# Graph attention on one core: overflow guard from softmax sums, and when a scheduling lead is given back

## Chip, cores, metric

The kernel runs on one core of a Trainium2 chip. The metric is the device time of one execution in microseconds, as the median of several runs. The engines are named TensorE (PE, with its weight loads as PEld), VectorE (DVE), ScalarE (ACT), GpSimd (POOL) and SyncE (SP, which here only issues DMAs).

## What is computed

One layer of graph attention with a residual and a layer norm, for 16 graphs (the batch) of 1024 nodes, 512 features, 8 heads of 64:

```python
q = (x @ Wq + bq).reshape(b, n, H, HD)
k = (x @ Wk + bk).reshape(b, n, H, HD)
v = (x @ Wv + bv).reshape(b, n, H, HD)
scores = jnp.einsum('bqhd,bkhd->bhqk', q, k) / jnp.sqrt(jnp.float32(HD))
scores = scores + (1.0 - adj)[None, None, :, :] * -1000000000.0
attn = jax.nn.softmax(scores, axis=-1)
out = jnp.einsum('bhqk,bkhd->bqhd', attn, v).reshape(b, n, d)
return _layernorm(x + out @ Wo + bo)
```

One adjacency matrix serves all graphs. It is sparse: an entry is 1 with a chance of about 0.004, more for early nodes. A query without any edge ("lone" below) has a softmax over 1024 equally masked scores; the kernel lets it take the mean of all values.

## The kernel before

**Edges instead of a score matrix.** The kernel sorts the queries by their number of edges (`ranks`, with the result in `asked_row` and `ranked`) and cuts them into 8 tiles of 128. Tile t handles its first `OWN[t]` = 1, 2, 2, 3, 4, 5, 5, 7 edges in "own" blocks, in which partition p is query p; the edges beyond that, of the two last tiles, are packed into 1 and 5 further blocks (`BLOCKS`), whose results are added by a matmul with a 0/1 matrix (`add_up`, lines 906 and 907). That is 29 + 6 = 35 blocks a graph, `NB` = 35, 560 in all, each with 128 edges.

**Front work**, in `pair` and `transpose_x`: x is loaded (SP), transposed on TensorE, multiplied by the weights; q goes to `q_rows` and k beside v to `kv_rows` in DRAM (SP), each of which has `ROWS` = 3 buffers, so that graph b overwrites graph b - 3. k and v come from a scheme with fewer products (lines 670 to 702). `norm` (line 566, ScalarE) squares and sums every row of q and k by pairs of heads, and `mean_pe` takes their maxima into `gmax` (line 623) and writes the mean of v into the extra row N of `kv_rows`.

**Attention work**, one block a step: POOL gathers q rows (line 824 or 834) and k and v rows (line 840) up to `AHEAD` = 8 blocks ahead; `products` (line 857, VectorE), `scores` (line 861, VectorE), `exponentials` (line 871, ScalarE; p is taken without subtracting a maximum), `weigh` (line 881 on ScalarE or line 885 on VectorE), `add_own` (line 897) or `add_up`. `normalise` divides by the sums of p at the end of a tile (lines 915 to 924), then comes a transpose on TensorE (line 932), a copy (936), and `finish`: projection by Wo (line 554), residual, layer norm (lines 762 to 784, with one power on POOL, line 778) and a scattering store (788).

**The order is written out by a planner** in the program, step by step[...]. A step n serves block n; there are 34 steps of lead-in before n = 0. Each step gets a `share` of TensorE time in microseconds, by costs: `PRODUCT` 0.86, `SUM` 0.87, `TRANSPOSE` 0.44. It is spent as `credit` on units of `finishing` (projections) first, and then of `fronts`, until the credit is used up. Functions put off by `later(k, fn)` and `later_last(k, fn)` run k steps on, in `plan` (before ScalarE's weighing) or `rest` (after it); transposes wait in `urgent` and go first. At each graph's first step the share is set so that, at the graph's end, front work is 2 graphs plus a lead ahead. The lead is `EARLY` = 13 steps, and `FIRST` = 11 more at the end of graph 0:

```python
                elif n % NB == 0:

                    left = sum(u[0] for u in fronts)
                    goal = fronts_time - (n // NB + 2 + (EARLY + (FIRST if n < NB else 0)) / NB) * batch_time
                    share = (max(0.0, left - goal) + NT * NPAIR * PRODUCT + NS * SUM) / NB
```

From step 455 on (graph 13) the remaining fronts are spread evenly up to step 513, and the ten tiles in `SPILL` (102 to 111) have their projections put off: their input goes to DRAM and comes back as `oTs` when the fronts are done. After that the share is `LAST_SHARE` = 3.0.

**The guard.** Since no maximum is subtracted, the kernel checks that the scores cannot be large: the greatest norm of q times (greatest norm of k + norm of bk) is at most `LIMIT`. It also checks (the tile `check`) that the matrix holds only 0 and 1 and that all edges fit into the blocks. `guard` runs as a generator, one piece a step from step 521 on, and writes `flag`. If the flag is set, a general program (`tile_general`) computes everything anew. Here it is not set.

Of the kernel before, what the change touches and what calls it, by code (L numbers as in the profile page):

```python
# [10 lines left out]
F32 = mybir.dt.float32  # L11
BF16 = mybir.dt.bfloat16
I32 = mybir.dt.int32
AF = mybir.ActivationFunctionType
OP = mybir.AluOpType
AX = mybir.AxisListType

HEADS = 8
EPS = 1e-5
NEG = 1e9  # L20
LIMIT = 31.0

# [8 lines left out]
LAZY = 2  # L33

SPILL = range(102, 112)
# [5 lines left out]
EARLY = 13  # L41

FIRST = 11
# [10 lines left out]
P = 128  # L54
# [103 lines left out]
def kernel(  # L158
# [32 lines left out]

    nc = tc.nc
    B, N, D = x.shape
    HD = D // HEADS
    NPAIR = D // P
    NT = N // P
    HALF = N // 2
    HD2 = D // 2  # L200
    scale = 1.0 / HD ** 0.5
# [23 lines left out]
    with ExitStack() as main:  # L225
# [6 lines left out]
        def fill_psum(name):  # L232
            return psum.tile([P, HALF], F32, tag="fill", name=name, bufs=4)
# [26 lines left out]
        query_row = one.tile([P, NS], I32, name="query_row")  # L260

        absent = one.tile([P, NB - NS], F32, name="absent")
        check = one.tile([P, 2 * NT], F32, name="check")

        asked, ranked = (one.tile([P, NT, 2], F32, name=name) for name in ("asked", "ranked"))
        key, rank = (one.tile([P, NT], F32, name=name) for name in ("key", "rank"))
        rank_row, asked_row = (one.tile([P, NT], I32, name=name) for name in ("rank_row", "asked_row"))
        ADJ = []
        gmax = one.tile([P, 2 * B], F32, name="gmax")

        kv_rows = [dram.tile([N + 1, 2 * D], F32, name=f"kv_rows_{i}") for i in range(ROWS)]
        q_rows = [dram.tile([N, D], F32, name=f"q_rows_{i}") for i in range(ROWS)]
# [42 lines left out]
        def bias_setup():  # L315
            bk_bc = work.tile([P, D], F32, tag="y", name="bk_bc", bufs=Y_BUFS)
            broadcast(bk_bc, bk)
            yield
            n4 = small.tile([P, NPAIR], F32, name="bk_norms")
            nc.vector.tensor_tensor(bk_bc, bk_bc, bk_bc, op=OP.mult)  # L320
            nc.vector.tensor_reduce(n4, bk_bc.rearrange("p (h d) -> p h d", d=P), axis=AX.X, op=OP.add)
            nc.vector.tensor_reduce(bk_norm, n4, axis=AX.X, op=OP.max)
            yield
            pb = fill_psum("pb")
            nc.tensor.transpose(pb[:, 0:2 * NPAIR], bias_rows, ident[:2 * NPAIR, :2 * NPAIR])
            nc.tensor.transpose(pb[:, 2 * NPAIR:3 * NPAIR], bv_rows, ident[:NPAIR, :NPAIR])
            yield
            nc.vector.tensor_copy(bias_qk, pb[:, 0:2 * NPAIR])
            bv_col = one.tile([P, NPAIR], F32, name="bv_col")
            nc.vector.tensor_copy(bv_col, pb[:, 2 * NPAIR:3 * NPAIR])  # L330
            bvb = work.tile([P, NPAIR, P], F32, tag="y", name="bvb", bufs=Y_BUFS)
            nc.vector.tensor_copy(bvb, bv_col[:, :, None].to_broadcast([P, NPAIR, P]))
            yield
            pb = fill_psum("pb3")
            for c in range(NPAIR):
                nc.tensor.matmul(pb, bvb[:, c, :], W["o"][:, c, :], start=(c == 0), stop=(c == NPAIR - 1))
            yield
            nc.vector.tensor_tensor(bo_bc, pb, bo_bc, op=OP.add)
# [5 lines left out]
        def later(k, fn):  # L344
            plan.setdefault(now[0] + k, []).append(fn)

        def later_last(k, fn):
            rest.setdefault(now[0] + k, []).append(fn)
# [3 lines left out]
        def ranks():  # L352
# [46 lines left out]
            yield  # L399
            yield  # L400
            nc.vector.tensor_copy(asked_row, ranked[:, :, 0])

        def checks():
            for t in range(NT):
# [153 lines left out]

            return [(PRODUCT, lambda c=c: unit(c), None) for c in range(NPAIR)]

        def norm(b, t, i, s):
            if t == 0 and i == 0:
                NRM[b] = work.tile([P, 2, NT, NPAIR], F32, tag="nrm", name=f"nrm_{b}", bufs=2)
            for h in range(NPAIR):
                sq = work.tile([P, P], F32, tag="sq", name=f"sq_{b}_{t}_{i}_{h}", bufs=2)
                nc.scalar.activation(sq, s[:, ts(h, P)], AF.Square, accum_out=NRM[b][:, i, t, h:h + 1])  # L566

        def pair(b, j):

# [7 lines left out]
            def out_q(i, p):  # L577

                assert gathered[0] >= NB * (b - ROWS + 1)
                q = work.tile([P, D], F32, tag="q", name=f"q_{b}_{tt[i]}", bufs=2)  # L580
                nc.vector.scalar_tensor_tensor(q, p, scale, bq_bc, op0=OP.mult, op1=OP.add)  # L581
                later(1, lambda: nc.sync.dma_start(q_rows[b % ROWS][ds(tt[i] * P, P), :], q))
                later_last(1, lambda: norm(b, tt[i], 0, q))

            def out_k(i, p):
                kv = new_kv(i)
                nc.scalar.copy(kv[:, 0:D], p)
                later_last(1, lambda: norm(b, tt[i], 1, kv[:, 0:D]))

            def out_v(i, p):  # L590
                nc.scalar.copy(KV[b, tt[i]][:, D:], p)
# [20 lines left out]
            def mean_pe():  # L612
                p = fill_psum(f"pm_{b}")
                nc.tensor.matmul(p[0:1, :], mean, VSUM.pop(b), start=True, stop=True)

                def out():
                    m = work.tile([1, D], F32, tag="q", name=f"mean_{b}", bufs=2)
                    nc.scalar.copy(m, p[0:1, :])
                    nc.sync.dma_start(kv_rows[b % ROWS][N:N + 1, D:], m)
                    set_up[b] = True  # L620
                    nrm = NRM.pop(b)
                    for i in range(2):
                        nc.vector.tensor_reduce(
                            gmax[:, i * B + b:i * B + b + 1], nrm[:, i, :, :], axis=AX.XY, op=OP.max
                        )

                later(1, out)

# [62 lines left out]
            def out_k1():  # L691
                kv = KV[b, tt[1]]
                nc.vector.tensor_tensor(kv[:, 0:D], R["p4"], R["g"], op=OP.add)
                send(1)
                later_last(1, lambda: norm(b, tt[1], 1, kv[:, 0:D]))

            def out_v1():
                nc.vector.tensor_tensor(new_kv(1)[:, D:], R["z"], R["g"], op=OP.add)  # L698
# [113 lines left out]

        KG, QG, PV, PSUM, QT = {}, {}, {}, {}, {}
        blocks = [(b, t, i) for b in range(B) for t in range(NT) for i in range(OWN[t] + BLOCKS[t])]

        def gather(n):
# [30 lines left out]

        def products(n):  # L850
            b, t, i = blocks[n]
            if i < OWN[t]:
                q = QT[b, t] if i < OWN[t] - 1 else QT.pop((b, t))
            else:
                q = QG.pop(n)
            QK[n] = work.tile([P, D], F32, tag="qk", name=f"qk_{n}", bufs=2)
            nc.vector.tensor_tensor(QK[n], q, KG[n][:, 0:D], op=OP.mult)  # L857
# [51 lines left out]
        def normalise(b, t):  # L909
            pv = PV.pop((b, t))  # L910
            o = work.tile([P, D], F32, tag="o", name=f"o_{b}_{t}", bufs=2)
            r = small.tile([P, HEADS], F32, tag="rden", name=f"rden_{b}_{t}", bufs=2)
            if BLOCKS[t]:
                s = PSUM.pop((b, t))
                nc.vector.tensor_tensor(r, s[:, 1, HD2:HD2 + HEADS], pv[:, D:], op=OP.add)
# [13 lines left out]
            def transpose():  # L929
# [12 lines left out]

                later(1, out)

            later(1, lambda: urgent.append(transpose))
            if not fronts:
                coming.append((b, t))
# [1 line left out]


        def guard():
            g = small.tile([P, 4], F32, name="g")
            for i in range(2):
                nc.vector.tensor_reduce(g[:, i:i + 1], gmax[:, ts(i, B)], axis=AX.X, op=OP.max)
            nc.vector.tensor_reduce(g[:, 2:3], check, axis=AX.X, op=OP.max)
            nc.vector.tensor_copy(g[:, 3:4], bk_norm)
            yield
            pg = fill_psum("pgt")
            nc.tensor.transpose(pg[0:4, 0:P], g, ident)
            yield  # L960
            m = small.tile([4, 1], F32, name="gm")
            nc.vector.tensor_reduce(m, pg[0:4, 0:P], axis=AX.X, op=OP.max)
            yield
            pg = fill_psum("pgt2")
            nc.tensor.transpose(pg[0:1, 0:4], m, ident[0:4, 0:4])
            yield
            r = small.tile([1, 8], F32, name="r")
            nc.vector.tensor_copy(r[:, 0:4], pg[0:1, 0:4])
            yield
            yield  # L970
# [11 lines left out]
            nc.vector.tensor_scalar(r[:, 4:5], r[:, 4:5], LIMIT, None, op0=OP.is_le)  # L982
            nc.vector.tensor_scalar(r[:, 5:6], r[:, 2:3], 0.0, None, op0=OP.is_le)
            nc.vector.tensor_tensor(r[:, 6:7], r[:, 4:5], r[:, 5:6], op=OP.mult)
            nc.vector.tensor_scalar(flag, r[:, 6:7], -1.0, 1.0, op0=OP.mult, op1=OP.add)

        out_rows = {(b, t): out_views[b * NT + t].rearrange("b n d -> (b n) d") for b in range(B) for t in range(NT)}
        done, coming, spilled, gathered, fronts = [], [], [], [0], []

        total = len(blocks)  # L990
        prep = {}
# [2 lines left out]
        prep.setdefault(12 - LEAD_IN, []).append(bias_setup())  # L994
        prep.setdefault(-22, []).append(checks())
        preps = [loads(), ranks()]
        prep.setdefault((B - 1) * NB - 4, []).append(guard())
        with tc.manual_schedule():

            fronts += transpose_x(0, 0) + transpose_x(0, 1)  # L1000
# [8 lines left out]
            for t in range(3):  # L1009
                load_x(0, t)  # L1010
            n = -LEAD_IN
            while n < total or plan or rest or urgent or done or finishing or spilled:
                now[0] = n
                if n < 0:
                    share = LISTS_SHARE if n > -16 else LEAD_SHARE if n > -LEAD_IN else TRANSPOSE * 1.5
                elif n >= SPILL[0] // NT * NB + NB:

                    share = sum(u[0] for u in fronts) / max(fronts_end - n, 1) + NS * SUM / NB if fronts else LAST_SHARE
                elif n % NB == 0:

                    left = sum(u[0] for u in fronts)
                    goal = fronts_time - (n // NB + 2 + (EARLY + (FIRST if n < NB else 0)) / NB) * batch_time
                    share = (max(0.0, left - goal) + NT * NPAIR * PRODUCT + NS * SUM) / NB
                if 0 <= n + 3 < total:
                    exponentials(n + 3)
# [31 lines left out]
                while credit > 0 or urgent:  # L1057
                    if urgent and not (first_unit and fronts):
                        urgent.pop(0)()
                        continue  # L1060
                    if not finishing and len(done) > (LAZY if fronts else 0) and n > loaded.get(done[0], n) + 1 and n > last_finish + 1:
                        finishing = finish(*done.pop(0))
                        last_finish = n
                    units = finishing or fronts
# [56 lines left out]
```

## Time and profile before

| | |
|---|---|
| median of 3 runs | 2012.16 us (2010.32 to 2013.15) |
| profiled execution | 2012.86 us |
| its span, first to last instruction | 2011.1 us |
| granted TensorE clock, mean | 0.988 |
| DMA: moved, mean rate | 563.17 MB, 280 GB/s |
| POOL gathers of k and v, line 840 | 560, 635.8 us busy, 453.5 us idle before them |
| ScalarE weighing, line 881 | 3608, 910.4 us |
| ScalarE squares of q and of k, line 566 | 512 and 512, 151.1 and 150.9 us |

The busy time of an engine counts its instructions, not its waits. Two instructions of one engine can overlap, so that the sum over a group can be more than the group's share of busy time. An fp32 matmul stands in the trace as two passes. Idle time is put down to what ended it.

### The profile page before, as it was taken

The page shows a single profiled execution, that of the slowest core. Times are in us where ns is not written, and L with a number is a line of the kernel's source. Part 1 is how long each engine was busy: PE and PEld are TensorE (multiplying, and loading weights), DVE is VectorE, ACT ScalarE, POOL GpSimd, SP SyncE. Part 2 cuts the span into 40 slices and gives each one's busy share as a digit, 9 for nine tenths or more (in the row PEclk, how much of TensorE's full clock was granted, in tenths as well). Part 3 has the DMA queues.
Part 4 walks back from the last instruction along what each step waited for, and adds up shares of the span by engine and source line. Part 5 has one row for each costly group of instructions (what it writes and reads, how often), then busy time and mean ns, then how long its engine had stood idle before and what let it go on. Part 6 is the DMA issues. An engine that isn't in the chain of part 4 may idle for free. (4 is left out here: it accounts for less than half of the span.)

```text
span 2011.1 us, 26727 instructions
## 1 busy us (share of the span) xinstructions
PE 1923.4 (96%) x5378; PEld 926.2 (46%) x5378; DVE 1785.5 (89%) x3653; ACT 1682.9 (84%) x7048; POOL 1303.5 (65%) x1224
## 2 busy tenths in 40 slices
PE   8988998899999999999999999999999999899885
PEld 4434453444445454454445445454444444444442
DVE  3799999899899998989899898999999998999784
ACT  4637989789897988979898898979898898989894
POOL 1673657767576675767667575767767575566784
PEclk9999999999999999999999999999999999999898
DMA  6697887878888796888879688887978788988883
GB/s 246 207 368 247 269 294 259 290 250 307 282 283 308 255 319 226 304 294 280 300 260 321 227 317 272 292 297 263 319 259 290 266 299 302 320 302 291 296 295 123
DMA packets 191148, 563.17 MB, mean 280 GB/s; under 512 B 31711, under 2 KB 31739, under 8 KB 190974
## 3 DMA queue, kind: packets, MB, share of 16 engines
q0 software_dynamic: 121632, 403.22, 60.0%
q1 hardware_dynamic: 66736, 153.16, 20.5%
q10 hardware_dynamic: 2606, 4.99, 0.7%
q14 instruction: 129, 1.06, 0.2%
q8 instruction: 45, 0.74, 0.1%
HBM read 442.25 MB, written 143.71 MB: 291 GB/s over the span
## 5 line engine op out<-in xcount | busy, mean ns | idle before, releaser
L840 POOL DMA_INDIRECT kvg<-kv_rows,key_row x560 | 635.8, 1135 | 453.5 <-ACT pv L871 142.9
L881 ACT ACTIVATE pv<-kvg,pv 128x64 f32<-128x64 f32 x3608 | 910.4, 343 | 0.0
L554 PE MATMUL pq<-wq,xT 128*128 128x512 f32 x1024 | 476.7, 595 | 3.1 <-DVE q L581 1.8
L554 PE MATMUL po<-wo,oT 128*128 128x512 f32 x944 | 443.4, 601 | 5.6 <-ACT oT L936 2.9
L861 DVE TENSOR_REDUCE s<-qk 128x8 f32<-128x512 f32 x560 | 381.5, 681 | 6.8 <-DVE qk L857 0.5
L857 DVE TENSOR_TENSOR qk<-qt,kvg 128x512 f32<-128x512 f32 x464 | 317.8, 685 | 12.0 <-DMA kvg<-kv_rows,key_row 11.8
L554 PEld LDWEIGHTS pq<-wq,xT 128*128 128x128 f32 x1024 | 192.8, 191 | 219.7 <-issue 196.1
L554 PEld LDWEIGHTS po<-wo,oT 128*128 128x128 f32 x944 | 176.3, 192 | 215.7 <-issue 193.5
L670 PE MATMUL pp<-t,s 128*128 128x512 f32 x504 | 237.2, 593 | 6.3 <-DVE s L540 6.3
L670 PE MATMUL x<-b,xT 128*128 128x512 f32 x504 | 238.9, 596 | 0.7 <-ACT e L683 0.7
L897 DVE TENSOR_TENSOR pv<-pv,pv 128x520 f32<-128x520 f32 x336 | 233.7, 695 | 1.5 <-ACT pv L881 1.5
L871 ACT ACTIVATE pv<-s,absent 128x8 f32<-128x8 f32 x464 | 137.1, 297 | 72.5 <-DVE s L861 39.0
L788 POOL DMA_INDIRECT out_dram<-y,asked_row x128 | 153.3, 1198 | 36.0 <-issue 16.3
L566 ACT ACTIVATE sq<-q 128x128 f32<-128x128 f32 x512 | 151.1, 302 | 23.7 <-DVE q L581 23.5
L824 POOL DMA_INDIRECT qt<-q_rows,asked_row x128 | 140.0, 1094 | 36.7 <-issue 31.9
L566 ACT ACTIVATE sq<-kv 128x128 f32<-128x128 f32 x512 | 150.9, 302 | 0.0
L670 PEld LDWEIGHTS x<-b,xT 128*128 128x128 f32 x504 | 95.9, 191 | 117.9 <-issue 110.8
L670 PEld LDWEIGHTS pp<-t,s 128*128 128x128 f32 x504 | 94.2, 190 | 112.7 <-issue 97.1
L724 POOL DMA_INDIRECT y<-in_x_dram,asked_row x102 | 115.5, 1132 | 30.0 <-issue 27.8
L834 POOL DMA_INDIRECT qg<-q_rows,query_row x96 | 107.2, 1117 | 27.5 <-issue 22.7
L670 PE MATMUL z<-t,s 128*128 128x512 f32 x252 | 120.0, 599 | 0.0
L670 PE MATMUL z<-b,s 128*128 128x512 f32 x252 | 118.6, 593 | 1.1 <-DVE kv L698 1.1
(173 smaller groups left out, 2802.0 us busy)
## 6 DMA issues: line engine op xcount, KB each, us to landing
kv_rows<-kv SPq DMA_DIRECT2D x128, 512.0 KB
x<-in_x_dram SPq DMA_DIRECT2D x128, 256.0 KB
q_rows<-q SPq DMA_DIRECT2D x128, 256.0 KB
kvg<-kv_rows,key_row POOLq DMA_INDIRECT x560, 6.0
residual<-y_sorted SPq DMA_DIRECT2D x26, 256.0 KB
y<-residual SPq DMA_DIRECT2D x26, 256.0 KB
adj<-in_adj_dram POOLq DMA_DIRECT2D x8, 512.0 KB, 12.7
spill<-oT SPq DMA_DIRECT2D x10, 256.0 KB
```

What stands on the lines that cost most here:

```text
L554: nc.tensor.matmul(p, lhs()[:, ts(c, P)], w[:, c, :], start=(c == 0), stop=(c == NPAIR - 1))
L566: nc.scalar.activation(sq, s[:, ts(h, P)], AF.Square, accum_out=NRM[b][:, i, t, h:h + 1])
L670: nc.tensor.matmul(R[bank], l[:, ts(c, P)], right[:, c, :], start=(first and c == 0), stop=(c == 1), skip_group_check=True,)
L724: nc.gpsimd.indirect_dma_start(out=y, out_offset=None, in_=x_rows, in_offset=bass.IndirectOffsetOnAxis(ap=asked_row[:, t:t + 1], axis=0), ...
L788: nc.gpsimd.indirect_dma_start(out=out_rows[b, t], out_offset=bass.IndirectOffsetOnAxis(ap=asked_row[:, t:t + 1], axis=0), in_=y, in_offse ...
L824: nc.gpsimd.indirect_dma_start(out=QT[b, t], out_offset=None, in_=q_rows[b % ROWS], in_offset=bass.IndirectOffsetOnAxis(ap=asked_row[:, t: ...
L840: nc.gpsimd.indirect_dma_start(out=KG[n], out_offset=None, in_=kv_rows[b % ROWS], in_offset=bass.IndirectOffsetOnAxis(ap=key_row[:, g:g + ...
L857: nc.vector.tensor_tensor(QK[n], q, KG[n][:, 0:D], op=OP.mult)
L861: nc.vector.tensor_reduce(S[n], QK.pop(n).rearrange("p (h d) -> p h d", d=HD), axis=AX.X, op=OP.add)
L871: nc.scalar.activation(PV[n][:, D:], S.pop(n), AF.Exp, bias=bias)
L881: nc.scalar.activation(pv[:, ts(h, HD)], v[:, ds(D + h * HD, HD)], AF.Copy, scale=pv[:, D + h:D + h + 1])
L897: nc.vector.tensor_tensor(PV[b, t], PV[b, t], pv, op=OP.add)
```

## The change

It has four parts.

1. *Guard.* Norms of q are no longer taken for all queries. They are taken for the first tile of each graph alone, from the gathered tile `qt`, and scaled by `lone`, which is 1 for a query without an edge and 0 for others. A new column of `check` sees that no lone query lies beyond the first tile. For all other queries the guard looks at the reciprocals of the sums of p (`RDEN`, kept for a whole graph): their least and greatest value per graph go into `ends` and must lie within `RANGE`. The last part of the guard therefore runs after the last block, and its first part starts four steps later than before (step 525).
2. *Lead.* The 11 steps of `FIRST` are kept until the end of graph 1 and given back in twelve equal parts over the following graphs.
3. *End.* No projection is started in the last two steps.
4. *Buffers.* Some small tiles have one buffer instead of two or four.

```diff
+RANGE = 1e-25, 1e25
...
-        check = one.tile([P, 2 * NT], F32, name="check")
+        check = one.tile([P, 2 * NT + 1], F32, name="check")
+
+        lone = one.tile([P, 1], F32, name="lone")
+        lone_norm = one.tile([P, B], F32, name="lone_norm")
+        ends = one.tile([P, 2, B], F32, name="ends")
...
+            yield
+            nc.vector.tensor_scalar(lone, ranked[:, 0, 1:2], 0.0, None, op0=OP.is_le)
+
+            nc.vector.tensor_scalar(check[:, 2 * NT:], ranked[:, 1, 1:2], 0.0, None, op0=OP.is_le)
...
-        def norm(b, t, i, s):
-            if t == 0 and i == 0:
-                NRM[b] = work.tile([P, 2, NT, NPAIR], F32, tag="nrm", name=f"nrm_{b}", bufs=2)
+        def squares(name, s, sums, scale=1.0):
             for h in range(NPAIR):
-                sq = work.tile([P, P], F32, tag="sq", name=f"sq_{b}_{t}_{i}_{h}", bufs=2)
-                nc.scalar.activation(sq, s[:, ts(h, P)], AF.Square, accum_out=NRM[b][:, i, t, h:h + 1])
+                sq = work.tile([P, P], F32, tag="sq", name=f"sq_{name}_{h}", bufs=2)
+                nc.scalar.activation(sq, s[:, ts(h, P)], AF.Square, scale=scale, accum_out=sums[:, h:h + 1])
...
-                later_last(1, lambda: norm(b, tt[i], 0, q))
...
-                    nrm = NRM.pop(b)
-                    for i in range(2):
-                        nc.vector.tensor_reduce(
-                            gmax[:, i * B + b:i * B + b + 1], nrm[:, i, :, :], axis=AX.XY, op=OP.max
-                        )
+                    nc.vector.tensor_reduce(gmax[:, b:b + 1], NRM.pop(b), axis=AX.XY, op=OP.max)
...
+            if t == 0 and i == 0:
+                norms = small.tile([P, NPAIR], F32, tag="lone", name=f"lone_{b}", bufs=1)
+                later_last(0, lambda q=QT[b, t]: squares(f"q_{b}", q, norms, lone))
+                later(2, lambda: nc.vector.tensor_reduce(lone_norm[:, b:b + 1], norms, axis=AX.X, op=OP.max))
...
-            r = small.tile([P, HEADS], F32, tag="rden", name=f"rden_{b}_{t}", bufs=2)
+            if t == 0:
+                RDEN[b] = small.tile([P, NT, HEADS], F32, tag="rden", name=f"rden_{b}", bufs=1)
+            r = RDEN[b][:, t, :]
...
+            if t == NT - 1:
+                r = RDEN.pop(b)
+                for k, op in enumerate((OP.min, OP.max)):
+                    nc.vector.tensor_reduce(ends[:, k, b:b + 1], r, axis=AX.XY, op=op)
...
-            nc.vector.tensor_scalar(flag, r[:, 6:7], -1.0, 1.0, op0=OP.mult, op1=OP.add)
+            while now[0] <= total:
+                yield
+
+            g = small.tile([P, 4], F32, name="gr", bufs=1)
+            for k, op in enumerate((OP.min, OP.max)):
+                nc.vector.tensor_reduce(g[:, k:k + 1], ends[:, k, :], axis=AX.X, op=op)
+                nc.vector.tensor_scalar(g[:, 2 + k:3 + k], g[:, k:k + 1], RANGE[k], None, op0=(OP.is_ge, OP.is_le)[k])
+            nc.vector.tensor_tensor(g[:, 0:1], g[:, 2:3], g[:, 3:4], op=OP.mult)
+            pg = fill_psum("pgt3")
+            nc.tensor.transpose(pg[0:1, 0:P], g[:, 0:1], ident)
+            yield
+            nc.vector.tensor_reduce(r[:, 7:8], pg[0:1, 0:P], axis=AX.X, op=OP.min)
+            nc.vector.tensor_tensor(r[:, 8:9], r[:, 6:7], r[:, 7:8], op=OP.mult)
+            nc.vector.tensor_scalar(flag, r[:, 8:9], -1.0, 1.0, op0=OP.mult, op1=OP.add)
+            guarded.append(True)
...
-        prep.setdefault((B - 1) * NB - 4, []).append(guard())
+        prep.setdefault((B - 1) * NB, []).append(guard())
...
-                    goal = fronts_time - (n // NB + 2 + (EARLY + (FIRST if n < NB else 0)) / NB) * batch_time
+                    ahead = EARLY + FIRST * (1 - max(0, n // NB - 1) / (SPILL[0] // NT))
+                    goal = fronts_time - (n // NB + 2 + ahead / NB) * batch_time
...
-                    if not finishing and len(done) > (LAZY if fronts else 0) and n > loaded.get(done[0], n) + 1 and n > last_finish + 1:
+                    if (
+                        not finishing and len(done) > (LAZY if fronts else 0) and n > loaded.get(done[0], n) + 1
+                        and n > last_finish + 1 and not total - 2 <= n < total
+                    ):
```

## The prediction, made before the changed kernel was run

> **What bounds the kernel now.** I read the busy shares first, then the same shares batch by batch, then TensorE's timeline where it pauses, then the waits of the two batches in which it pauses again, and the end. The overall shares say TensorE:
>
> ```profile
> PE 1923.4 (96%) x5378; PEld 926.2 (46%) x5378; DVE 1785.5 (89%) x3653; ACT 1682.9 (84%) x7048; POOL 1303.5 (65%) x1224
> ```
>
> 96% is an average. I cut the span at the start of every 35th score reduction (DVE, line 861): 35 steps are one batch. Columns: stretch, length, then busy time (and count) of PE, PEld, DVE, ACT, POOL, then TensorE's granted clock, DMA share, GB/s. The rows are batch 0, 1, 2, 4, 12, 13, 14, 15.
>
> ```profile
> 146.10:274.70 128.60, 122.18 (x347) 59.44 (x346) 121.52 (x261) 103.85 (x454) 66.19 (x64) 0.97 0.80 274
> 274.70:384.60 109.90, 94.39 (x255) 44.34 (x254) 98.80 (x202) 96.70 (x407) 78.50 (x72) 0.95 0.81 268
> 384.60:499.00 114.40, 113.13 (x321) 54.16 (x320) 105.79 (x218) 100.07 (x418) 81.02 (x73) 1.00 0.83 284
> ...
> 617.20:733.30 116.10, 116.10 (x331) 56.55 (x330) 107.88 (x220) 101.69 (x431) 81.01 (x73) 1.00 0.83 285
> ...
> 1551.60:1667.70 116.10, 116.10 (x331) 56.50 (x330) 108.09 (x219) 100.75 (x430) 78.86 (x71) 1.00 0.83 283
> 1667.70:1770.70 103.00, 94.95 (x277) 45.35 (x275) 95.43 (x172) 94.66 (x432) 62.04 (x53) 1.00 0.89 313
> 1770.70:1878.60 107.90, 104.14 (x287) 49.18 (x287) 100.33 (x206) 93.39 (x395) 66.28 (x63) 1.00 0.89 307
> 1878.60:1976.80 98.20, 84.08 (x220) 40.10 (x218) 80.94 (x206) 87.10 (x313) 79.08 (x84) 0.93 0.82 281
> ```
>
> Batches 2 to 12 take 1283.1 us, 116.6 each, and TensorE is busy in all but 5.0 us of them: TensorE's work is their price. Batch 1 is different: TensorE idles 15.5 us of 109.9, at clock 0.95. There the planner hands out less front work, since it takes back the first 11 of 24 steps of lead at once. TensorE then waits for others and is slow after a wait:
>
> ```profile
> 371.59 1.88 PE L670 MATMUL z<-b,s 128*128 128x512 f32 x4
> 379.11 1.22 PE L906 MATMUL sum<-pv,sums 128*128 128x256 f32 x2 [5.64 <-DVE pv L885]
> ...
> 381.01 3.62 PE L670 MATMUL x<-b,xT 128*128 128x512 f32 x4
> ```
>
> Four matmuls take 3.62 us after the 5.64 us pause, 1.88 before it. In batches 13 and 14 it idles 8.0 and 3.8 us; there gathers come late because POOL waits for buffers that ScalarE has not freed (in us: total, times, longest):
>
> ```profile
> POOL kvg L840 <- ACT pv L871: 23.2, 11, 4.2
> ...
> DVE qk L857 <- DMA kvg<-kv_rows,key_row: 6.6, 4, 2.6
> ```
>
> [...]
>
> **The change, part by part.** The sum is made against the profiled execution: 2012.86 us, a span of 2011.1 and 1.8 around it, 0.7 above the median 2012.16.
>
> *1. The lead given back over twelve batches.* Front work of a batch is 88 products of 0.86 and 8 transposes of 0.44, 79.2 us (four 0.43 us passes start 1.72 us apart in the timeline, so the planner's 0.86 is what the chip does). The 11 steps are 11/35 x 79.2 = 24.9 us. Before, batch 1 did that much less; after, it does a full share, and each of batches 2 to 13 does 2.07 us less. Batch 1 after: 94.4 busy, less the half clock (0.97 and 0.93 in the two windows of 50 us that cover it, 1.5 + 3.5 = 5.0 us), plus 24.9, plus 1.2 idle as in batch 2, is 115.5 instead of 109.9: **+5.6**. Batches 2 to 12, bound by TensorE: 11 x 2.07 = **-22.8**. Net **-17.2**. The next bound is near: VectorE is busy 108 us a batch, below the new 114.5. Ends: batch 1 as long as the longest batch, 118.2, gives -14.5; with no idle left -18.5. Moved with the fronts go their x loads and the q_rows and kv_rows stores on SP, and POOL's gathers meet them. A store of batch m+2 overwrites batch m-1; with 24 steps of lead it comes at step 11 of batch m, and the last gather of m-1 was issued 8 steps before batch m: 19 steps, over 60 us, lie between. I cost the order at nothing.
>
> *2. Squares of q removed, four per batch put back.*
>
> ```profile
> L566 ACT ACTIVATE sq<-q 128x128 f32<-128x128 f32 x512 | 151.1, 302 | 23.7 <-DVE q L581 23.5
> ```
>
> With its accumulator read a square holds ScalarE for about 0.31 us (72 in batch 13: 22.1 us). 512 go, 156 us; 64 come back at 0.31 + 0.09, 26 us: ScalarE loses 130 us, 8 a batch. In batches 2 to 12 this lies beside TensorE and is worth at most the 5.0 us of idle: I take **-1**, ends -4 and 0. In lead-in and batch 0 VectorE and the loads are late: 0, ends -2 and +1. In batches 13 and 14 it counts. TensorE, VectorE and ScalarE are there within 1 us of each other (95, 95.4, 94.7 of 103.0), so each waits for the others. 11 us less of ScalarE in batch 13 frees gather buffers sooner and answers VectorE's 6.6 us. Also TensorE has 2 us less there. VectorE cannot go under its 195.8 busy of 210.9. I take **-4.5**, about two thirds of that wait, ends -10 and 0. The new squares wait for the gathered qt tile in ScalarE's queue, with the next exponentials and weighings behind them; VectorE's product waits for the same gather and a later one first, so 0, ends 0 and +2.
>
> *3. VectorE's additions.* 16 reduces of 0.18 us (line 623) go, 16 small ones and 32 of 128x64 come (0.16 to 0.25 each by lines 954 and 962): +6 us over the run, 0.4 a batch, under TensorE's cover in 1 to 12; where the cover is gone, in 13 and 14, 0.8 us, counted in the -4.5. The two comparisons in the lists' set-up: 0.3 us, 0.
>
> *4. The end.* TensorE in order of time:
>
> ```profile
> 1979.79 0.59 PE L906 MATMUL sum<-pv,sums 128*128 128x256 f32 x2
> 1980.22 0.61 PE L907 MATMUL sum<-pv,sums 128*128 128x264 f32 x2
> 1980.66 1.88 PE L554 MATMUL po<-wo,oTs 128*128 128x512 f32 x4
> ...
> 1984.96 0.59 PE L906 MATMUL sum<-pv,sums 128*128 128x256 f32 x2
> 1985.39 0.61 PE L907 MATMUL sum<-pv,sums 128*128 128x264 f32 x2
> 1987.69 0.66 PE L932 MATMUL poT<-ident,o 128*128 128x128 f32 x4 [1.69 <-DVE stats L768]
> 1989.13 3.58 PE L554 MATMUL po<-wo,oT 128*128 128x512 f32 x4 [0.79 <-ACT oT L936]
> ```
>
> A projection of 4.3 us stands ahead of the last sum, whose input has been ready since VectorE's 1979.55. After: sum at 1980.7, that projection to 1985.8 while VectorE normalises (2.0 us), transposes to 1986.4, last projection from about 1987.5 instead of 1989.1 and perhaps at full clock. It ended at 1995.3 and ends at 1991.8: **-3.5**, ends -4.5 and 0. The guard's second half adds, at step 561, seven VectorE operations of about 0.15 us and one transpose on TensorE that waits for them; behind it stands the last projection. That is the 1.1 us between transposes and projection, and is in the sum. Its last three operations and the flag come before the last statistics: 0. Moving the guard's first half four steps later moves nine POOL operations (3.6 us from 1903.6 on) with a gather behind them: 0, ends -1 and +1.
>
> Sum: -17.2 - 1 - 4.5 - 3.5 = -26.2, so 2012.9 - 26.2 = 1986.7: **1987 us**.
>
> **Rivals.** *Only the lead pays.* Batch 1 keeps its stalls (POOL's gather ahead of line 778, VectorE behind it) and lasts 118 to 120, ScalarE's relief changes nothing and the end gains 1: -14 - 1 = 1998. For it: those stalls are not TensorE's. Against: batch 2 has the same work and 1.3 us of idle. *All covers go.* -18.5, -8 in batches 13 and 14, -4 in 2 to 12, -1 in the lead-in, -4.5 at the end: 1977. For it: ScalarE appears in most of POOL's waits. *Slower.* The lead is not given back, because batches 2 to 12 have a second bound at 116.6: VectorE's 108 plus its waits for POOL and ScalarE. Then batch 1 costs its 5.6 and nothing returns: 2018.5. It decides if that floor is over 116.1 us a batch (11 x 0.5 = 5.6). Against: in batches 4 and 12 TensorE has no idle at all; and of VectorE's 8.8 us of idle a batch (1283.1 less 1185.8 busy, by 11) 3.0 are waits for TensorE (33.5 us in all), which shrink with TensorE's work, so the floor stands at about 113.6. *It does not do what it says:* were the flag set, the general program would run after all this; for these inputs all conditions have room, and I give it less than 1 in 100.
>
> **How the numbers follow.** Forecast 1987 (1981 to 1994): 0.55. Only the lead, 1998 (1994 to 2006): 0.24. All covers, 1977 (1970 to 1981): 0.12. Slower: 0.05. The rest, 0.04, lies near no change. A measurement can tell 0.2%, 4 us, from no change; the first three cases lie beyond it, so faster 0.91, same 0.04, slower 0.05. The range 1976 to 2002 leaves out the lower part of the third case, the slow part of the second and the last two, under 2 in 10.
>
> **What would show it.** Right: batch 1 at about 115.5 with TensorE full at clock 1.00; batches 2 to 12 at about 114.5, still without idle; ScalarE's busy time near 1550; in batches 13 and 14 VectorE's wait for gathers down and 4 us less; the last two sums ahead of the last spilled projection. Wrong: idle TensorE in batches 2 to 12, or stalls of batch 1 that stay under full front work.

## The result, and the profile after

The changed kernel takes 1982.8 us in the median (1980.1 to 1986.5, 4 runs) beside 2011.3 us for the kernel before: a ratio of 0.9859, 95% interval 0.9837 to 0.9880, or 28.5 us less. The forecast was 1987 (1981 to 1994). The profiled execution took 1980.1 us, with a span of 1978.3; it is the fastest of the four.

The busy shares, as in the first view of before:

```profile
PE 1913.1 (97%) x5379; PEld 925.0 (47%) x5379; DVE 1785.8 (90%) x3694; ACT 1566.4 (79%) x6152; POOL 1301.4 (66%) x1224
```

ScalarE lost 116.5 us of busy time, VectorE's is the same. TensorE's is 10 us less with one matmul more. About 6 of it is put down to batch 1, by an estimate: it took up 24.9 us of front work by the forecast's count and is busy only 18.9 us longer (113.3 against 94.4), at clock 1.00 where it was 0.95 before. The batches again, cut at every 35th score reduction (here line 874); columns as before the change. The rows are batch 1, 4, 12, 13 and 14:

```profile
273.40:389.70 116.30, 113.30 (x320) 54.64 (x318) 105.91 (x218) 98.61 (x398) 77.23 (x72) 1.00 0.82 274
...
615.80:728.30 112.50, 112.50 (x320) 54.54 (x319) 105.81 (x217) 90.53 (x361) 77.75 (x72) 1.00 0.85 289
1532.40:1646.60 114.20, 114.20 (x326) 55.65 (x325) 107.68 (x221) 95.17 (x379) 79.94 (x75) 1.00 0.87 302
1646.60:1744.20 97.60, 91.83 (x269) 44.94 (x267) 94.08 (x171) 86.19 (x368) 56.14 (x50) 0.98 0.92 318
1744.20:1851.00 106.80, 103.38 (x286) 49.32 (x287) 100.43 (x209) 87.56 (x353) 64.84 (x61) 1.00 0.88 304
```

Batches 2 to 12 as one row, before and then after:

```profile
384.60:1667.70 1283.10, 1278.15 (x3621) 620.29 (x3620) 1185.80 (x2407) 1126.45 (x4778) 870.17 (x801) 1.00 0.83 284
```

```profile
389.70:1646.60 1256.90, 1255.94 (x3562) 610.18 (x3563) 1178.68 (x2417) 1042.76 (x4146) 876.41 (x804) 1.00 0.85 289
```

Batch 1 is longer now, but full: TensorE idles 3.0 us instead of 15.5, and its clock is 1.00. Batches 2 to 12 follow at 114.3 us each, with 1.0 us of idle TensorE in all. Where TensorE had stood 5.64 us before a sum and then ran at half clock (four matmuls in 3.62 us), it now stands 0.26 us before the same sum and stays at full clock (four in 1.88 us; TensorE in order of time):

```profile
382.89 0.70 PE L919 MATMUL sum<-pv,sums 128*128 128x256 f32 x2 [0.26 <-DVE pv L898]
...
383.88 1.88 PE L679 MATMUL pp<-t,s 128*128 128x512 f32 x4
```

VectorE still stands ahead of that sum, 2.18 us for POOL's power. Before, it stood 2.89 us:

```profile
376.31 0.16 DVE L781 TENSOR_TENSOR stats<-stats 128x1 f32<-128x1 f32 x1 [2.89 <-POOL stats L778]
```

The difference is that TensorE now has front work to do meanwhile (12 passes of line 679 in a row from 377.33 us on, 1.88 us for each four).

At the end, both sums come first, and the projection that stood between them follows (TensorE in order of time):

```profile
1951.68 0.59 PE L919 MATMUL sum<-pv,sums 128*128 128x256 f32 x2
...
1952.55 1.88 PE L565 MATMUL po<-wo,oTs 128*128 128x512 f32 x4
...
1956.85 0.60 PE L947 MATMUL poT<-ident,o 128*128 128x128 f32 x4
1958.53 0.27 PE L1013 MATMUL pgt<-ident,gr 128*1 128x128 f32 x1 [1.08 <-DVE stats L777]
1958.64 1.88 PE L565 MATMUL po<-wo,oT 128*128 128x512 f32 x4
```

The last four-matmul group starts at full clock (1.88 us, 3.58 before). The guard's transpose makes TensorE wait 1.08 us ahead of it.

The stages of six profiled executions, in us of span. "After, again" is a second execution of the changed kernel (experiment 9). "Lead", "guard" and "end" are the three parts of the change, each made alone (experiments 1 to 3):

| stage | before | forecast of the change | after | after, again | lead alone | guard alone | end alone |
|---|---|---|---|---|---|---|---|
| lead-in | 146.1 | 0 | 144.6 | 144.1 | 145.9 | 144.4 | 144.3 |
| batch 0 | 128.6 | 0 | 128.8 | 128.7 | 128.6 | 127.8 | 128.6 |
| batch 1 | 109.9 | +5.6 | 116.3 | 116.4 | 117.5 | 106.5 | 110.0 |
| batches 2 to 12 | 1283.1 | -22.8 - 1 | 1256.9 | 1256.8 | 1261.9 | 1279.2 | 1283.0 |
| batches 13, 14 | 210.9 | -4.5 | 204.4 | 206.1 | 206.4 | 210.2 | 210.2 |
| batch 15 | 98.2 | 0 | 96.8 | 98.0 | 100.4 | 96.2 | 100.3 |
| after that | 34.3 | -3.5 | 30.5 | 32.2 | 32.7 | 33.0 | 30.1 |
| span | 2011.1 | -26.2 | 1978.3 | 1982.3 | 1993.4 | 1997.3 | 2006.5 |

Batch 15 ends at the last score reduction, so it is 34 steps and not 35. The table also gives the scatter. "End alone" changes nothing in the lead-in and is 1.8 us shorter there, and the two executions of the changed kernel differ by 1.7 us in batches 13 and 14 and by 1.7 us in the last stage. Differences of less than 2 us in one stage of one execution therefore prove little by themselves.

### The profile page after: what moved, and what is told of

The parts are those of the page before. It is cut to its first block, busy times and chain, and to the rows that moved or that the text cites. A ratio compares the mean times of both kernels' runs of the same rounds, so it can differ in the third digit from the quotient of the medians.

```text
span 1978.3 us, 25784 instructions
## 1 busy us (share of the span) xinstructions
PE 1913.1 (97%) x5379; PEld 925.0 (47%) x5379; DVE 1785.8 (90%) x3694; ACT 1566.4 (79%) x6152; POOL 1301.4 (66%) x1224
## 5 line engine op out<-in xcount | busy, mean ns | idle before, releaser
L565 PE MATMUL po<-wo,oT 128*128 128x512 f32 x944 | 437.0, 595 | 4.7 <-DVE y L771 1.9
L575 ACT ACTIVATE sq_k<-kv 128x128 f32<-128x128 f32 x512 | 150.7, 299 | 8.8 <-DVE kv L702 8.8
L733 POOL DMA_INDIRECT y<-in_x_dram,asked_row x102 | 117.2, 1149 | 30.6 <-issue 28.5
L679 PE MATMUL pp<-t,xT 128*128 128x512 f32 x252 | 118.4, 592 | 0.0
```

Source lines behind the costliest of these rows:

```text
L565: nc.tensor.matmul(p, lhs()[:, ts(c, P)], w[:, c, :], start=(c == 0), stop=(c == NPAIR - 1))
L575: nc.scalar.activation(sq, s[:, ts(h, P)], AF.Square, scale=scale, accum_out=sums[:, h:h + 1])
L679: nc.tensor.matmul(R[bank], l[:, ts(c, P)], right[:, c, :], start=(first and c == 0), stop=(c == 1), skip_group_check=True,)
L733: nc.gpsimd.indirect_dma_start(out=y, out_offset=None, in_=x_rows, in_offset=bass.IndirectOffsetOnAxis(ap=asked_row[:, t:t + 1], axis=0), ...
```

## The experiments

**1 to 3. Each part alone.** The edits are the hunks of the diff: the two lines of `ahead` and `goal`; everything that concerns the guard, the norms and their buffers; the condition with `total - 2`. The buffers (part 4 of the change) go with the guard and were not tried alone.

> The kernel before with the lead given back over twelve batches, and nothing else. Theory A (the lead fills batch 1 by itself): 16 to 19 us less than before; batch 1 at about 116 us with TensorE idle 1 to 3 us and clock 1.00, batches 2 to 12 together 20 to 23 us shorter. Rival B (batch 1 fills only when ScalarE is relieved of the squares of q too): batch 1 stays above 119 us with 5 us or more of idle TensorE, and the gain is 8 to 13 us.

Measured: 1996.9 us beside 2012.3, ratio 0.9918 (0.9904 to 0.9933), 15.4 us less. Batch 1 and batches 2 to 12 (one row), then 13 and 14:

```profile
274.50:392.00 117.50, 113.53 (x320) 54.68 (x318) 106.20 (x217) 105.56 (x452) 78.28 (x73) 1.00 0.83 273
392.00:1653.90 1261.90, 1257.77 (x3563) 610.32 (x3564) 1176.77 (x2394) 1120.26 (x4741) 874.63 (x803) 1.00 0.85 288
1653.90:1751.10 97.20, 91.66 (x268) 44.98 (x267) 93.93 (x171) 92.83 (x426) 55.94 (x50) 0.98 0.89 310
```

The lead fills batch 1 by itself, with all of ScalarE's squares still there (105.6 us busy): clock 1.00, 4.0 us idle. The next eleven batches are 21.2 us shorter. Rival B falls. Theory A holds in its mechanism, a little under its range in the whole and with 1 us more idle than its 1 to 3. Batches 1 to 12 together give 13.6 us. The third row was not foreseen: batch 13 is 5.8 us shorter than before (103.0), though ScalarE got no relief; batch 14 is 1.3 us longer.

> The kernel before with the new guard alone (no squares of q but for the first tile of each graph, last part of the guard after the last block); lead and end as before. Theory A: 7 to 11 us less: batches 2 to 12 lose their 5 us of idle TensorE, batches 13 and 14 lose 4 to 6 us, batch 1 up to 2 us. Rival C (ScalarE's squares, not the lead, made the stalls of batch 1): batch 1 alone loses 8 us or more and the gain is 15 to 20 us, so that lead and guard overlap. Rival D (relief without the longer lead only moves idle time): 0 to 3 us less.

Measured: 2000.8 us beside 2012.3, ratio 0.9939 (0.9925 to 0.9952), 11.5 us less. The rows are batch 1, batches 2 to 12, and 13:

```profile
272.20:378.70 106.50, 92.58 (x258) 44.23 (x257) 98.51 (x205) 92.53 (x369) 76.99 (x71) 0.97 0.83 275
378.70:1657.90 1279.20, 1276.81 (x3618) 620.30 (x3617) 1186.97 (x2428) 1048.26 (x4170) 871.38 (x802) 1.00 0.84 285
1657.90:1757.70 99.80, 94.18 (x277) 45.68 (x275) 95.40 (x173) 86.61 (x370) 61.20 (x51) 1.00 0.92 317
```

The size is near that of theory A, the place is not. Batch 1 gives 3.4 us, batches 2 to 12 give 3.9. Batch 13 is 3.2 us shorter, but batch 14 is 2.5 longer, so that both together give 0.7 where A had 4 to 6. In batch 14 the clock is 0.98, and the same 287 matmul passes are busy 1.9 us longer, so by estimate some 2 us of that are the clock's and not the guard's. Rivals C and D fall. These stages give 8.0 of the 13.8 us by which the profiled span is shorter. The rest lies where nothing was forecast (lead-in 1.7, batch 0 0.8, batch 15 2.0, the end 1.3), and each of these is within the scatter.

VectorE's wait for gathers in batches 13 and 14, which was 6.6 us before, with the lead alone and then with the guard alone (us in total, times, longest):

```profile
DVE qk L857 <- DMA kvg<-kv_rows,key_row: 2.3, 3, 1.8
```

```profile
DVE qk L870 <- DMA kvg<-kv_rows,key_row: 4.0, 2, 2.4
```

So each part takes a share of that wait, the lead the greater one. In both executions of the whole change it is gone.

> The kernel before with no projection started in the last two steps, and nothing else. Theory A: 3 to 4 us less, all behind the last sum: the last sum at about 15.5 us before the last store's issue instead of 15.2 plus 4.3, the last projection at full clock. Rival (the delayed projection is as late for the end as the sum was): no change.

Measured: 2009.4 us beside 2012.3, ratio 0.9985 (0.9974 to 0.9996), 2.9 us less: just under A's range, and the rival's "no change" lies just outside the interval. The last stage of the table falls by 4.2 us and batch 15 grows by 2.1, in which the change does nothing before its last two steps. Together with the three parts' medians, 15.4 + 11.5 + 2.9 = 29.8, against 28.5 for the whole: they add up within what the runs can tell.

**4. How near the next bound is.** In the changed kernel:

```diff
-                nc.tensor.matmul(p, lhs()[:, ts(c, P)], w[:, c, :], start=(c == 0), stop=(c == NPAIR - 1))
+                if not (name.startswith("po_") and c in (1, 2) and 2 * NB <= now[0] < 13 * NB):
+                    nc.tensor.matmul(p, lhs()[:, ts(c, P)], w[:, c, :], start=(c == 0), stop=(c == NPAIR - 1))
```

> The changed kernel with two of the four products of each output projection left out from step 70 to step 454, so that some 14 us of TensorE's work a batch is missing in batches 2 to 12 and the attention is projected with half of its features there; everything else stands in its place. It measures the bound that the other engines set. Theory A (TensorE sets the length of batches 2 to 12, others stand at about 111 to 114): these batches fall to 109 to 113 us, bound by VectorE at 107 busy, with TensorE idle 8 to 12 us each. Rival E (a second bound at 114 or more, so that giving the lead back there soon stops paying): they stay at 113.5 or more. If nothing but TensorE mattered they would fall to 100.

Batches 2 to 12 in one execution, with TensorE's busy time cut by 121 us (11 a batch, where some 14 were meant):

```profile
389.60:1611.30 1221.70, 1134.89 (x3214) 543.41 (x3215) 1173.52 (x2417) 1041.51 (x4145) 881.75 (x803) 0.99 0.87 297
```

1221.7 / 11 = 111.1 us a batch, of which VectorE is busy 106.7. Before, these batches took 116.6, and after, 114.3. TensorE idles 7.9 us a batch, VectorE 4.4. So TensorE did set them, and the others stand 3.2 us or more below the new length. Theory A holds but for one point: VectorE is not busy throughout, so its work alone is not that bound. Rival E falls, and so does the rival that ended on the slow side, a second bound at 116.6, by 5.5 us a batch.

**5. Lead and end with the old guard.**

> The changed kernel with the guard of before (squares of q for all queries, guard from step 521 on), so lead and end together. Theory A (the parts add up but for batch 1, whose stalls lead and guard both take away): 18 to 19 us less than before, and the guard is worth 9 to 11 us on top. Rival (they overlap by the 3.4 us that the guard alone took from batch 1): 20 to 22 us less, and the guard is worth 7 to 8 on top.

Experiments 5 to 8 ran on a chip where the kernel before took 2025.6 us, so only ratios within them are compared: 0.9914 (0.9887 to 0.9941), 16.4 us less. Experiment 8, which has the new guard too, stands beside it 10.2 us lower. The 16.4 lies below both ranges, while its interval (12 to 23 us) holds both; the 10.2 lies in A's. So A is the nearer one, but the rival is not excluded.

**6, 7 and 10. How much of the lead is left for batches 13 and 14.** Of the 11 steps, the changed kernel has 11/12 of a step left when batch 13 starts. In it, `/ (SPILL[0] // NT)` (that is 12) was replaced by `/ 11`, which leaves none, and by `/ 24`, which leaves nearly 6.

> The changed kernel with the 11 steps given back in eleven parts, so that none is left when batch 13 starts (one step, 2 us of TensorE's work, was left). It asks why batches 13 and 14 became shorter with the lead alone. Theory F (the rest of the lead left for them, which takes front work out of a stage where engines wait for each other): batches 13 and 14 go back from 204.4 to 207 or more, batches 2 to 12 are 2 us shorter, and the kernel is 0 to 3 us slower than the changed one. Rival G (chance of the order there): batches 13 and 14 stay within 1.5 us of 204.4 and the kernel is 1 to 2 us faster.

> The changed kernel with the 11 steps given back in twenty-four parts, so that 6 of them are still there when batch 13 starts. Batches 2 to 12 get 11 us longer in every theory (5 more steps of 2.26 us each). Theory F: batches 13 and 14 are 9 us or more shorter than 204.4, and the kernel is within 3 us of the changed one. Rival G (only VectorE's part of the front work, 0.4 of it, comes back in those batches): they are 3 to 6 us shorter, and the kernel is 5 to 8 us slower than the changed one.

Beside experiment 8, on the same chip: none left gives 2010.4 against 1999.0 us, with batches 13 and 14 at 211.2 against 206.2, but 2 to 12 are also 4.8 us longer, and 15 is 3.9. (The profiled execution of none left took 2016.6 us, 6 more than its median.) Half left gives 2009.0 us: 2 to 12 are 13.4 us longer, 13 and 14 are 5.4 shorter. Batch 13 with half left:

```profile
1676.30:1770.70 94.40, 82.42 (x236) 39.63 (x235) 93.42 (x170) 82.16 (x352) 60.80 (x51) 0.97 0.92 322
```

VectorE is busy 93.4 of 94.4 us there, so only 1 us of waiting is left to gain. The 5.4 us lie in G's range and F's 9 us or more falls, but the way is not G's: VectorE's own work in batch 13 shrank by only 0.8 us (94.2 in experiment 8), while its idle time fell from 5.2 to 1.0 us. The loss is 10 us, more than G's 5 to 8. For "none left", the first theory had the sign and not the size, so it was run again beside the changed kernel, on a chip at 2012.8 us for the kernel before.

> The changed kernel once more, to stand beside the three others on one chip. Same ratio as before, 0.984 to 0.988.

> The 11 steps given back in eleven parts, once more, beside the changed kernel on one chip, since the first time stood on a chip where single stalls of some us came and went. Theory F (the step left for batch 13 is worth more there than it costs before): batches 13 and 14 are 3 to 6 us longer than those of the changed kernel beside it, and the kernel is 1 to 4 us slower. Rival G: within 1.5 us of it in those batches, and 1 to 2 us faster in all. If it is over 8 us slower again, neither is the whole cause.

The changed kernel: 1984.5 us (1983.4 to 1985.4), ratio 0.9859. None left: 1988.2 us (1986.9 to 1989.1), ratio 0.9877, so 3.7 us slower. Batch 13 in the two:

```profile
1646.00:1743.70 97.70, 91.89 (x269) 44.99 (x267) 94.15 (x172) 86.28 (x368) 56.12 (x50) 0.98 0.92 317
```

```profile
1645.90:1746.40 100.50, 93.48 (x277) 45.49 (x275) 95.55 (x174) 88.32 (x379) 63.05 (x51) 1.00 0.91 317
```

Eight more passes of front work on TensorE (277 against 269) make batch 13 2.8 us and batch 14 1.6 us longer (the clock of batch 14 is 0.98 in both). In batches 2 to 12 TensorE is busy 2.2 us less, and the stage is only 0.5 us shorter (1256.3 against 1256.8). Theory F holds: the last step of lead is worth 4.4 us in 13 and 14 (5.0 between experiments 6 and 8).

**8. The guard's last part behind the last projection.**

```diff
-            while now[0] <= total:
+            while now[0] <= total + 3:
```

> The changed kernel with the last part of the guard three steps later, so that its transpose stands behind the last projection on TensorE and no longer ahead of it. Theory A: the 1.1 us that TensorE waited there go, 0.5 to 1.2 us less than the changed kernel. Rival (the flag comes so late now that the end waits for it): the same or up to 2 us slower.

Ratio 0.9860 (0.9831 to 0.9890), against 0.9859 for the changed kernel on other chips. The expected microsecond is below what these runs can tell: inconclusive. In the trace the last projection follows 1.27 us behind the start of the transposes instead of 1.79. TensorE still waits 0.67 us there, for the copy of `oT`, so about 0.5 us of the 1.08 was the guard's.

**11. What is ScalarE's time worth now?** In the changed kernel the calls of `norm` for k and the reduce into `gmax` are left out, so that the guard lacks the norms of k:

```diff
-                later_last(1, lambda: norm(b, tt[i], kv[:, 0:D]))
...
-                    nc.vector.tensor_reduce(gmax[:, b:b + 1], NRM.pop(b), axis=AX.XY, op=OP.max)
```

> The changed kernel without the squares of k as well (the guard then has no norm of k, the rest of the work is as before): another 150 us less on ScalarE. It asks what ScalarE's time is worth now. Theory A (TensorE sets batches 2 to 12, and batches 13 and 14 are bound by VectorE and the front work, not by ScalarE): 0 to 3 us less. Rival H (ScalarE is a second bound, and each 130 us of it brings 10 us as in the guard alone): 7 to 12 us less.

Measured: 1981.9 us, 2.6 less than the changed kernel beside it (ratio 0.9846, 0.9832 to 0.9859). Batch 13:

```profile
1646.20:1743.90 97.70, 91.87 (x269) 44.79 (x267) 94.17 (x171) 76.14 (x297) 57.51 (x50) 0.98 0.92 316
```

ScalarE is busy 76.1 instead of 86.3 us in it, and the batch takes 97.7 us as in experiment 9. Theory A holds and rival H falls: the first 116 us off ScalarE brought about ten, the next 141 (1566.7 to 1425.6 busy) bring 2.6.

**12. A try at batch 15.** Experiment 8 with `k = 5 if fronts else 8` for `k = 5 if fronts else 6` in `finish`.

> The changed kernel with the last part of the guard behind the last projection, and, once the fronts are done, the layer norm's shift and output two steps later, so that VectorE has its queue free for the products while POOL takes the power. In batch 15 VectorE waited 11.2 us for POOL there, and TensorE 11.1 us for VectorE. Theory A: VectorE's wait falls under 5 us, batch 15 from 96.8 to 91 to 94 us, and the kernel is 3 to 6 us faster than the changed one. Rival (the y buffers, held two steps longer, keep the next projections back): no change or slower by up to 3 us.

Measured: 1987.4 us, 3.0 more than the changed kernel beside it. The waits from batch 15 on, first the changed kernel's, then this one's (us in total, times, longest):

```profile
DVE stats L790 <- POOL stats L787: 10.9, 9, 2.8
```

```profile
PE po L565 <- ACT oT L951: 4.8, 3, 3.0
DVE stats L790 <- POOL stats L787: 4.5, 2, 3.6
```

VectorE's wait went as meant, and new ones took its place: TensorE waits 4.8 us for the copies of `oT` (1.6 in the changed kernel) and 2.0 for a spilled tile to come back (none). Work also moved behind the last score reduction: 51 matmul passes stand there instead of 38, and that stage takes 35.5 us instead of 32.2. That is the rival's outcome; whether the y buffers are behind it, as the rival has it, the waits do not say. No run gave a version that is faster than the changed one and keeps the whole guard.

## Why the prediction was right

**Step 1, the lead, -17.2: right in mechanism, short in size.** In the whole change batch 1 grew by 6.4 (forecast 5.6), and TensorE's busy time in batches 2 to 12 fell by 22.2 us (forecast 22.8). Made alone, the lead gave +7.6 and -21.2, so -13.6 in the stages it was priced for; its median of 15.4 also holds the 4.5 us of batches 13 and 14. By number that is the -14 of "Only the lead pays". That rival fails on the mechanism: it kept batch 1 at 118 to 120 with its stalls, and TensorE's stalls went (4.0 us idle with the lead alone, 15.5 before). VectorE's stalls behind POOL stayed in part (2.2 of 3.8 us), but TensorE no longer waits for them.

**Step 2, the squares, -1 and -4.5: too small in all, and in the wrong place.** The guard alone brought 11.5 us in the median, and 10.2 on top of lead and end, where these two terms have 5.5. In batches 2 to 12, the 5.0 us of idle TensorE fell to 1.0 us, four times what I took and at the end of its range. In batches 13 and 14 the forecast gave ScalarE's relief 4.5 us, about two thirds of VectorE's wait for gathers. That step is wrong. The wait did fall, but the length hardly followed: the guard alone brought 0.7 us there (some 2 more by estimate at clock 1.00 instead of 0.98 in batch 14), and 2.0 or 0.3 on top of the lead (206.4 to 204.4 or 206.1), while the lead alone brought 4.5. I had named the lead's remainder ("TensorE has 2 us less there") and given it no price of its own. Withdrawn in experiment 10, it costs 4.4 us. Three engines were within 1 us of each other there, and I drew from that that any of them would do. The front work loads two of them, TensorE and VectorE; the squares load ScalarE, and in experiment 11 another 10 us off ScalarE left the length of batch 13 as it was.

**Step 2, batch 1.** The guard alone took 3.4 us from it, and 1.2 on top of the lead. In the forecast this was left out, since the lead covers it.

**Steps 2 and 3, the work itself.** ScalarE lost 116.5 us and not 130. No run shows the forecast's 0.09 us as the price of a scale pointer in general. What the traces show is that the new squares, with theirs, take 388 ns in the mean against 302 for those of q before, 86 more, and that before the change line 871 took 297 ns with its bias pointer and 201 without. VectorE's 6 us more came to 2.8 with the guard alone (1788.3 against 1785.5).

**Step 4, the end, -3.5: right in mechanism, its size within the scatter.** The last stage fell by 3.8 us in one execution of the whole change and by 2.1 in the other, and by 4.2 with the end alone; in the median the end alone brought 2.9 (0.8 to 5.2). TensorE's wait for the guard is the 1.1 us that the forecast had, of which experiment 8 leaves about 0.5 to the guard.

**The guard's first part moved by four steps: 0 forecast, open.** Batch 15 took 98.2, 100.4 and 100.3 us with the old guard, and 96.8, 96.2 and 98.0 with the new one, about 2.6 less in the mean (97.8 and 97.1 in experiments 10 and 11). The runs of one guard differ by up to 2.2 us among these, and on the chip of experiments 5 to 8 the old guard took 101.1 and the new one 97.7, 99.0 and 101.6. So a gain is likely but not shown. Besides this shift the new guard has only a few small operations in that batch. Which of them it is, was not tried.

**The sum was lucky in part.** Measured alone, lead and end brought 2.4 us less than forecast, and the guard 6.0 more. These misses pull against each other, so the forecast of the whole is nearer than its terms. It is luck, too, that batches 13 and 14 gave the -4.5 at all: the lead brought it, not the squares. Where the guard's gain outside batches 1 to 12 comes from stays open.

**Right by its own test.** TensorE full in batch 1 at clock 1.00, batches 2 to 12 at 114.3 (forecast 114.5), ScalarE at 1566 (forecast near 1550), VectorE's wait for gathers in batches 13 and 14 gone and these 6.5 or 4.8 us shorter (forecast 4), the two sums ahead: all five signs were seen. The idle time that would have refuted it, in batches 2 to 12, fell to 1 us.

## What to carry to other kernels

Cut the span at the stages of the schedule before you believe a busy share: at 96% TensorE, batch 1 still had 15.5 us of idle TensorE and the eleven batches after it 5.0 together, and work taken out of the full stage and put into the hole gained the hole, plus what half clock behind it had cost (3.62 us for four matmuls instead of 1.88). Relief of an engine that is not the bound paid here while others waited for it, and then nearly stopped (about 10 us for the first 116 us taken off ScalarE, 2.6 for the next 141), so find the bound behind it by leaving work out, as in experiment 4. Where several engines are equally late, price what loads two of them ahead of what loads one: here one step of front work was worth 4.4 us, and the squares of q 0.3 to 2.0.

## What was not expected of the hardware

The same program varied from 1980.1 to 1986.5 us. In two profiled executions of it, batch 14 took 106.8 and 108.4 us with the same number of matmuls. TensorE's clock was 1.00 in the first and 0.98 in the second: a stretch at half clock fell into it that the other did not have. Both have the same pause ahead of the same eight passes (the first execution, then the second):

```profile
1781.57 3.70 PE L565 MATMUL po<-wo,oT 128*128 128x512 f32 x8 [1.88 <-DVE y L771]
```

```profile
1781.03 5.40 PE L565 MATMUL po<-wo,oT 128*128 128x512 f32 x8 [1.88 <-DVE y L771]
```

The difference of 1.70 us is about that of the two batches (1.6). A pause of 1.88 us was thus followed by half clock in one execution and not in the other. In the second execution the same happened at the end, behind a pause of 1.87 us ahead of the last sums (up to 1.06 and 1.08 us for two passes, 0.59 and 0.61 in the first), and its last stage is 1.7 us longer. In the kernel before, a pause of 1.87 us stands there too, and the sums behind it run at full clock (0.59 and 0.61 us).

On the chip of experiments 5 to 8, batch 0 took 134 to 136 us instead of 128.8. In experiment 8 TensorE stood 8.5 us there, before a matmul that waited for nothing that the profile shows, in a window in which the DMA engines were full (share 1.02), and then ran at half clock, four matmuls in 3.78 us (TensorE in order of time):

```profile
149.06 3.78 PE L565 MATMUL pq<-wq,xT 128*128 128x512 f32 x4 [8.47 <-issue]
```

The cause was not found. Full DMA engines alone do not make it: the changed kernel in its first execution has a share of 1.03 in the same 10 us, and TensorE is busy 9.2 of them.
